# A gated layer with quantised down projection on one core: a planner with chance and room, weight ranges by sums of absolute values, and a shorter rounding of the down weights

## The chip, the cores and the metric

The kernel runs on one core of a Trainium2 chip. A core has five engines that work side by side and meet at semaphores: TensorE (PE) multiplies matrices, and its loads of stationary operands (PEld) overlap the multiplications; VectorE (DVE), ScalarE (ACT) and GpSimd (POOL) work on elements; SyncE (SP) issues transfers between the chip's memory and the on-chip buffer. Each engine takes its own instructions in the order in which they were emitted. Results of TensorE land in eight banks of an accumulator memory (PSUM), which the other engines read.

The metric is the device time of one execution in microseconds, smaller is better. Three runs of the kernel before took 744.97, 745.54 and 746.1; their median is 745.54.

## What is computed

The reference, cut to what matters (B = 4 batches of S = 1024 tokens, D = 512, FF = 2048, C = 128):

```python
scale = cond @ norm_w.T + 1.0
ms = jnp.mean(x * x, axis=-1, keepdims=True)
h = x * (scale[:, None, :] * jax.lax.rsqrt(ms + EPS))
u = h @ up_w.T
val, gate = jnp.split(u, 2, axis=-1)
h = val * jax.nn.gelu(gate, approximate=False)
hq = h + jax.lax.stop_gradient(act_quant(h) - h)            # 127 / max|h| of a token, rounded
wq = down_w + jax.lax.stop_gradient(weight_quant(down_w) - down_w)   # -1, 0 or 1 by the mean of |w|
y = hq @ wq.T
return y + x
```

So each token is normalised, goes through a gated layer, has its 2048 values rounded to whole numbers by its own largest value, and is multiplied with a matrix of -1, 0 and 1.

## The kernel before

**Tiles.** The 2048 rows of the hidden layer are 16 tiles of 128 (index `j`), each with a gate and a value half of `up_w`. Tokens of a batch are two halves of 512. A slot `g = 16 b + j` is one row tile of one batch. The up products are done in 16-bit floats, each operand split into a high and a low part (`w_high`, `w_low`, `s_high`, `s_low`, `Tokens.high`, `Tokens.low`). Batch 0 uses the plain product (`plain`, `plain_half`, L886; the very first is `plain_first`, L929); later batches use seven products of half size with sums of blocks (`product`, L871, called from `slot`). The down product uses the same scheme in `Pair` (L1142) and, for the last batch, a plain one (`down_mm`, L1091).

**Preparing weights.** While batch 0 is computed, each row tile of `up_w` is loaded into H (`w_load`, L570 and L573), its range is found (`w_largest`, L578: the largest absolute value of each row; `w_factor`, L456 to L587: down to a power of two, a factor and its reciprocal), it is scaled (`w_scale`: GpSimd L606 for tiles 0 to 5, ScalarE L604 for tiles 6 to 15), and turned, either by TensorE through banks po (`w_turn`, L614, evacuated by `w_high`, `w_low`, `w_evac`) or, from tile 6 on, by a transposing transfer (`w_rows`, L628 to L630). GpSimd forms the sums of blocks (`s_sums`, L662 to L665), ScalarE and GpSimd split them (L674, L678), and SyncE stores them in memory (L682), from where later batches load them again. A row's factor only has to be a power of two that keeps the parts inside the 16-bit range; `gain` takes it out again.

`down_w` is loaded in eight pieces (`d_load`, L729), summed in absolute value by ScalarE (`d_sum`, L733), and rounded to -1, 0, 1: VectorE takes two steps (`d_round`, L748 and L749) and ScalarE writes the result as 8-bit floats (`d_put`, L758); a transposing transfer puts them into `wd` (L760), and VectorE forms block sums (`d_sums`, L771).

**A slot.** In batch 0 a half is: a gate product into bank A or B, Gelu by ScalarE (L910), a value product into bank E, their product by VectorE into H (L914), which frees bank E. In later batches a slot has six products in banks A, B and E, copies of A and E by ScalarE (L949, L957, L961), two Gelus (L966, L982) and sums by VectorE (L969, L979, L985, L988). VectorE keeps a running largest value of each token over pairs of tiles (`pair_max`: L1000, L1005, L1007).

**Change of batch.** When a batch's last pair is in, GpSimd takes the maximum over partitions (`token_max`, L1021, an all-reduce, with an empty one ahead of it, `get_ready`, L1014), VectorE makes the scale from it (`token_scale`: L1026, four reciprocals L1032 for each half), and 16 pieces are scaled and rounded (`quant_scale`, L1063; `quant_round`, L1067, or ScalarE L1071 and L1075), in the first half of the next batch's slots. Meanwhile the next tokens are squared, scaled and split (`Tokens.norm`, L805, L775, L776; `Tokens.scale`, L813, L815).

**The planner.** No engine call is emitted where it is written. `Engine` records it, and `Plan` adds it as a step with its dependences (by the parts of tiles that it reads and writes), a price (`price`) and, for a transfer, a time on the DMA engines. `Plan.order` repeats 24 times: `needed` works back from the end to when each step is due, `place` puts the steps, earliest due first, into the first room on their engine, and `replay` runs the resulting order through the prices. The order with the earliest end of TensorE is emitted, engine by engine. So a change of a price or of a rule of the planner can move every instruction of the kernel.

Of the kernel before, what the change touches and what calls it, by code (L numbers as in the profile page):

```python
# [21 lines left out]
P = 128  # L22
# [5 lines left out]

W_UP = 2.0**12
X_UP = 2.0**8  # L30

# [79 lines left out]
class Plan:  # L111


    def __init__(self):
        self.steps = []
        self.wrote, self.read = {}, {}
        self.loaded = {}
        self.lines = {}
# [5 lines left out]
    def add(self, eng, method, real, args, kwargs):  # L124
# [48 lines left out]
        s.deps = deps  # L173
        self.steps.append(s)

    def order(self):

        steps = self.steps
        for s in steps:
            s.after, s.cost = [], (s.alone + s.beside) / 2  # L180
        for s in steps:
            for d in s.deps:
                steps[d].after.append(s)
        clock = 0.0
        for s in steps:
            if s.eng == "PE":
                s.start = clock
                clock += s.cost
        best = None
# [17 lines left out]
    def place(self):  # L207

        steps = self.steps
        used = {e: Line() for e in ("PE", "ACT", "DVE", "POOL", "SP", "DMA")}  # L210
        last = 0.0
# [12 lines left out]
    def replay(self, order):  # L224

# [3 lines left out]
        for s in order:  # L229
# [11 lines left out]
            s.cost = (s.cost + cost) / 2 if e in port else cost  # L241
            free[e] = s.end
            if s.wait:
                free["DMA"] = max(free["DMA"], t + ISSUE) + s.wait
                s.end = free["DMA"] + LANDING
        return free["PE"]

# [6 lines left out]

ROUNDS, ISSUE, LANDING, RELOAD = 24, 1.2, 1.5, 6.5

# [28 lines left out]
def price(eng, method, writes, reads, args, kwargs):  # L285
# [72 lines left out]
def glu_quant_kernel(  # L358
# [34 lines left out]
    DVE.memset(one, 1.0)  # L393
    ones = one.to_broadcast([P, P])


# [42 lines left out]
    )  # L439
    A21 = R[:, 0, 6144 : 6144 + 768].bitcast(F16).rearrange("p (n w f) -> p n w f", n=3, w=2)  # L440

    def s_tile(g):
# [132 lines left out]
    def w_largest(j, t0=0, t1=2):  # L575
        t = slice(t0, t1)
        am = sm.tile([P, 2], F32, name=f"wam_{j}_{t0}", tag="wam")[:, t]
        DVE.tensor_reduce(am, wn(j)[:, t], AX.X, ALU.max, apply_absolute_value=True)  # L578
# [167 lines left out]
    def d_round(n):  # L746
        dn = d_part(n)
        DVE.tensor_scalar(dn, dn, wsc, 1.0, ALU.mult, ALU.min)  # L748
        DVE.tensor_scalar(dn, dn, -1.0, MAGIC, ALU.max, ALU.add)  # L749

    tn = []

    def d_put(n):
# [3 lines left out]
        t8 = tn[-1].bitcast(F8).rearrange("p (f y) -> p f y", y=2)  # L757
        ACT.activation(t8[:, :, y], d_part(n), AF.Copy, bias=-MAGIC, saturate=False)  # L758
        if y:
# [1118 lines left out]
```

## Time and profile before

| | before |
|---|---|
| median of three runs | 745.54 us |
| profiled execution, its own time | 746.14 us |
| its span in the trace | 744.4 us |
| ScalarE, VectorE, GpSimd busy | 392.7, 606.1, 210.5 us |
| DMA: read and written | 58.93 MB and 23.09 MB |
| DMA: packets under 512 bytes | 141750 of 179567 |

The profiled execution's own time is 1.7 us longer than its span, for what lies around the program. Rows of groups read: line, engine, operation, output and input with their shapes, count, then the busy time in us, the mean duration in ns, and the idle time of the engine just before them with what ended it. Rows of a timeline read: start, duration, engine, line, operation, shapes, count, and in brackets the idle time of the engine before it and what ended that. A matmul's duration holds its way through the pipeline, so successive ones overlap.

### The profile page before, as it was taken

What the parts mean: (1) busy time and instruction counts of PE and PEld (TensorE: products, weight loads), DVE (VectorE), ACT (ScalarE), POOL (GpSimd) and SP (SyncE); (2) the same over time, 40 slices, a digit from 0 to 9 for tenths busy, and PEclk for the clock granted to TensorE, in tenths of its full rate; (3) what the DMA queues carried; (4) which work ended last, traced back from release to release, by engine and by line L of the source; (5) the groups of instructions that cost most, each with busy time, mean ns of one, the idle gap of its engine ahead of it and who ended that gap; (6) DMA issues with size and microseconds to landing.
All of it is one profiled execution on the core that took longest, in us unless ns stands there. A gap on an engine that the chain in (4) does not pass through costs nothing.

```text
span 744.4 us, 10218 instructions
## 1 busy us (share of the span) xinstructions
PE 725.6 (97%) x3684; PEld 362.5 (49%) x3684; DVE 606.1 (81%) x833; ACT 392.7 (53%) x635; POOL 210.5 (28%) x213
## 2 busy tenths in 40 slices
PE   6999999999979999999999999999999999999997
PEld 3544444444434445666444445566444444445744
DVE  6787899988988887977587888988579889755897
ACT  5787576565225688333334678623333665332363
POOL 1775887857223034300015003800001000000000
PEclk9999999999999999999999999999999999999999
DMA  9838688899423454768733454676833344443514
GB/s 305 334 87 267 226 222 220 194 248 233 139 68 99 125 138 120 176 178 193 202 101 100 100 131 124 161 199 153 192 122 102 100 103 104 107 103 89 153 48 151
DMA packets 179567, 115.74 MB, mean 155 GB/s; under 512 B 141750, under 2 KB 147767, under 8 KB 179516
## 3 DMA queue, kind: packets, MB, share of 16 engines
q1 hardware_dynamic: 179226, 114.76, 57.5%
q10 hardware_dynamic: 290, 0.33, 0.3%
q8 instruction: 29, 0.48, 0.3%
q14 instruction: 22, 0.18, 0.1%
HBM read 58.93 MB, written 23.09 MB: 110 GB/s over the span
## 4 chain that ended last, share of the span: by engine, by line
PE 78%; DVE 9%; POOL 4%; issue 3%; ACT 3%; DMA 1%; SPq 0%; DVEq 0%; POOLq 0%; ACTq 0%
PE A L871 31%; PE E L871 15%; PE po L1142 8%; PE B L871 8%; PE E L886 5%; PE B L886 2%; PE A L886 2%; PE po L1091 2%; PE E L1091 1%; PE A L1091 1%; DMA H<-in_x_dram 1%; DVE H L629 1%; POOL H L663 1%; DVE nx L854 1%; DVE wam L578 1%
## 5 line engine op out<-in xcount | busy, mean ns | idle before, releaser
L871 PEld LDWEIGHTS <-SXY 128*128 128x128 f16 x2016 | 197.3, 98 | 237.1 <-issue 5.8
L871 PE MATMUL A<-R,SXY 128*128 128x512 f16 x1152 | 266.4, 379 | 3.7 <-ACT t L949 1.6
L871 PE MATMUL E<-R,SXY 128*128 128x512 f16 x576 | 140.0, 379 | 0.8 <-DVE t L979 0.8
L1021 POOL PARTITION_ALL_REDUCE am<-R x8 | 18.9, 2364 | 304.3 <-DVE R L1007 286.4
L1063 DVE TENSOR_TENSOR H<-H,am 128x1024 f32<-128x1024 f32 x64 | 78.3, 1256 | 0.2
L886 PEld LDWEIGHTS <-SXY 128*128 128x128 f16 x462 | 45.2, 98 | 55.6 <-issue 2.1
L969 DVE SCALAR_TENSOR_TENSOR H<-A,sg,t 128x512 f32<-128x512 f32 x48 | 35.9, 749 | 43.0 <-PE A L871 42.9
L871 PE MATMUL B<-R,SXY 128*128 128x512 f16 x288 | 70.0, 379 | 0.0
L1005 DVE TENSOR_REDUCE gm<-H 128x512 f32<-128x1024 f32 x56 | 69.0, 1232 | 1.0
L982 ACT ACTIVATE t<-t,sg 128x512 f32<-128x512 f32 x48 | 34.7, 722 | 54.6 <-DVE t L979 54.6
L949 ACT COPY t<-A 128x512 f32<-128x512 f32 x48 | 28.1, 585 | 60.0 <-PE A L871 60.0
L1142 PE MATMUL po<-wd,R 128*128 128x256 fp8e4 (+1 forms) x448 | 56.8, 275 | 0.8 <-ACT po L1168 0.8
L957 ACT COPY B<-A 128x512 f32<-128x512 f32 x48 | 27.4, 570 | 51.4 <-PE A L871 51.4
L1142 PEld LDWEIGHTS <-R 128*128 128x128 bf16 (+1 forms) x480 | 47.0, 98 | 13.9 <-issue 1.3
L985 DVE TENSOR_TENSOR v<-A,v 128x512 f32<-128x512 f32 x48 | 33.2, 691 | 24.9 <-PE A L871 22.4
L966 ACT ACTIVATE t<-B,sg 128x512 f32<-128x512 f32 x48 | 33.0, 687 | 32.6 <-PE B L871 32.0
L886 PE MATMUL E<-R,SXY 128*128 128x512 f16 x210 | 49.9, 379 | 0.0
L979 DVE TENSOR_TENSOR t<-E,t 128x512 f32<-128x512 f32 x48 | 33.0, 687 | 20.4 <-PE E L871 19.7
L886 PEld LDWEIGHTS <-R 128*128 128x128 f16 x282 | 27.5, 98 | 34.4 <-issue 2.0
L1071 ACT ACTIVATE H<-H 128x1024 f32<-128x1024 f32 x38 | 40.0, 1051 | 7.5 <-DVE H L1063 7.3
L961 ACT COPY v<-E 128x512 f32<-128x512 f32 x48 | 28.1, 586 | 28.4 <-PE E L871 21.5
L1007 DVE TENSOR_TENSOR R<-R,gm 128x512 f32<-128x512 f32 x56 | 40.4, 722 | 1.4
(232 smaller groups left out, 1036.9 us busy)
## 6 DMA issues: line engine op xcount, KB each, us to landing
SXY<-s_dram SPq DMA_DIRECT2D x66, 256.0 KB, 2.7
SXY<-s_dram SPq DMA_DIRECT2D x18, 384.0 KB, 3.9
H<-in_L_cond_up_w_dram SPq DMA_DIRECT2D x13, 512.0 KB, 5.5
s_dram<-SXY SPq DMA_DIRECT2D x14, 384.0 KB, 4.0
xr<-in_x_dram SPq DMA_DIRECT2D x19, 256.0 KB, 3.7
out_dram<-xr SPq DMA_DIRECT2D x19, 256.0 KB, 2.0
H<-in_x_dram SPq DMA_DIRECT2D x8, 512.0 KB, 5.3
R<-in_L_cond_down_w_dram SPq DMA_DIRECT2D x8, 512.0 KB, 7.4
```

The lines of the kernel that those rows point to most:

```text
L871: PE.matmul(o, s[:, w, k, :], tv[:, :, c, l, k, :], start=start and n == 0, stop=stop and n == len(TERMS) - 1, skip_group_check=True,)
L886: PE.matmul(ps, a[k // 2][:, w, k % 2, :], XP[:, l, k, h * TOK : (h + 1) * TOK], start=n == 0, stop=n == len(terms) - 1,)
L966: ACT.activation(cur["t1"], pb, AF.Gelu, scale=gain(g, 1))
L969: DVE.scalar_tensor_tensor(h_half(g - 1, 0), prev["A"], gain(g - 1, 0), prev["t1"], ALU.mult, ALU.mult)
L979: DVE.tensor_tensor(prev["t2"], prev["E"], prev["t2"], ALU.add)
L982: ACT.activation(prev["t2"], prev["t2"], AF.Gelu, scale=gain(g - 1, 1))
L985: DVE.tensor_tensor(cur["v"], cur["A"], cur["v"], ALU.add)
L1005: DVE.tensor_reduce(gm[0], v, AX.X, ALU.max, apply_absolute_value=True)
L1007: return [largest, lambda: DVE.tensor_tensor(m, m, gm[0], ALU.max)]
L1063: DVE.tensor_tensor(v, v, r.to_broadcast([P, 2, TOK]), ALU.mult)
L1071: ACT.activation(v, v, AF.Copy, bias=MAGIC)
L1142: PE.matmul(po, w[:, j], m, start=start and j == 0, stop=stop and j == n - 1, skip_group_check=True,)
```

## The change

Five things change.

- `w_largest` for tiles 6 to 15 (`BY_SUM`): instead of one VectorE reduction to the largest absolute value, two ScalarE activations write the absolute values of 512 elements to a scratch place and give their sum; the factor in `w_factor` is doubled for them (`W_UP_SUM`).
- `d_round`: VectorE multiplies and adds the rounding constant in one step, with no clamps; `d_put` takes the sign after subtracting the constant, instead of a copy.
- Planner, dependences: among the first 150 steps (`HEAD`) each step that is not a transfer follows the one written before it on its engine.
- Planner, placing: TensorE's steps may go into room between others; other steps are placed with some room after their inputs (0, 0.3, 0.6 or 0.9 us in turn, at most a tenth of what they have until due); a transfer's place is found on the DMA engines first. Among 25 rounds the order is chosen by the mean end over four replays in which costs (TensorE's apart) and landings are drawn at random, and the end is that of all steps.
- Planner, prices: ScalarE, GpSimd and VectorE prices are adjusted a little.

The diff, cut to its core:

```diff
@@ add
+        if not s.wait:
+            if s.n < HEAD and eng in self.last:
+                deps.add(self.last[eng])
+            self.last[eng] = s.n
@@ order
+        best, chance = None, random.Random(1)
         for n in range(ROUNDS):
             self.needed(clock)
-            self.place()
+            self.place(0.3 * (n % 4))
             order = sorted(steps, key=lambda s: (s.start, s.n))
             clock = self.replay(order)
-            if best is None or clock < best[0]:
-                best = clock, order
+            late = sum(self.replay(order, chance) for _ in range(MISSES)) / MISSES
+            if best is None or late < best[0]:
+                best = late, order
+            self.replay(order)
@@ needed
-            s.late = clock if s.eng != "PE" else s.start
+            s.late = s.start if s.eng == "PE" else clock - s.cost
@@ place
-            if s.eng == "PE":
-                t = max(t, last)
-                last = t + s.cost
-                s.start, s.end = t, last
-                continue
+            if s.eng != "PE":
+                t += min(margin, max(0.0, s.late - t) * 0.1)
+            if s.wait and s.eng == "SP":
+                t = used["DMA"].put(t + ISSUE, s.wait) - ISSUE
             s.start = used[s.eng].put(t - s.before, s.before + s.cost) + s.before
-            s.end = s.start + s.cost
-            if s.wait:
-                s.end = used["DMA"].put(s.start + ISSUE, s.wait) + s.wait + LANDING
+            s.end = s.start + (ISSUE + s.wait + LANDING if s.wait else s.cost)
@@ replay
+            if chance:
+                cost *= 1.0 if e == "PE" else 0.95 + 0.14 * chance.random()
+            else:
+                s.cost = (s.cost + cost) / 2 if e in port else cost
...
-        return free["PE"]
+        return max(s.end for s in order)
...
+HEAD = 150
+ROUNDS, MISSES, ISSUE, LANDING, RELOAD = 25, 4, 1.2, 1.5, 6.5
@@ price
-        cost = 0.06 + wide * 0.0009 + (0.07 if method != "copy" else 0)
+        cost = 0.08 + wide * 0.0009 + (0.05 if method != "copy" else 0) + (0.05 if psum else 0)
...
-        return cost, cost * 1.33, 0.0
+        return cost, cost * 1.42, 0.0
...
-    return cost, cost * (1.35 if method == "scalar_tensor_tensor" else 1.65), 0.0
+    return cost, cost * (1.35 if method == "scalar_tensor_tensor" else 1.8), 0.0
@@ w_largest, w_factor
+        if j >= BY_SUM:
+            for n in range(t0, t1):
+                ACT.activation(w_junk, wn(j)[:, n], AF.Abs, accum_out=am[:, n : n + 1])
+            return am
         DVE.tensor_reduce(am, wn(j)[:, t], AX.X, ALU.max, apply_absolute_value=True)
...
-        DVE.tensor_scalar(sw[:, j, t], am, 2.0**-100, 1.0 / W_UP, ALU.max, ALU.mult)
+        up = W_UP_SUM if j >= BY_SUM else W_UP
+        DVE.tensor_scalar(sw[:, j, t], am, 2.0**-100, 1.0 / up, ALU.max, ALU.mult)
@@ d_round, d_put
-        DVE.tensor_scalar(dn, dn, wsc, 1.0, ALU.mult, ALU.min)
-        DVE.tensor_scalar(dn, dn, -1.0, MAGIC, ALU.max, ALU.add)
+        DVE.tensor_scalar(dn, dn, wsc, MAGIC, ALU.mult, ALU.add)
...
-        ACT.activation(t8[:, :, y], d_part(n), AF.Copy, bias=-MAGIC, saturate=False)
+        ACT.activation(t8[:, :, y], d_part(n), AF.Sign, bias=nmagic, saturate=False)
```

More of the change, by code (lines that the diff above doesn't have):

```diff
@@ L1 @@
 import bisect
+import random
 import sys
@@ L29 @@
 W_UP = 2.0**12
+BY_SUM = 6
+W_UP_SUM = 2.0**13
 X_UP = 2.0**8
@@ L116, in __init__ @@
         self.wrote, self.read = {}, {}
-        self.loaded = {}
+        self.loaded, self.last = {}, {}
         self.lines = {}
@@ L188, in order @@
                 clock += s.cost
-        best = None
+        best, chance = None, random.Random(1)
         for n in range(ROUNDS):
             self.needed(clock)
-            self.place()
+            self.place(0.3 * (n % 4))
             order = sorted(steps, key=lambda s: (s.start, s.n))
             clock = self.replay(order)
-            if best is None or clock < best[0]:
-                best = clock, order
+            late = sum(self.replay(order, chance) for _ in range(MISSES)) / MISSES
+            if best is None or late < best[0]:
+                best = late, order
+            self.replay(order)
         self.replay(best[1])
@@ L202, in needed, with place, replay @@
         for s in reversed(self.steps):
-            s.late = clock if s.eng != "PE" else s.start
+            s.late = s.start if s.eng == "PE" else clock - s.cost
             for t in s.after:
                 s.late = min(s.late, t.late - lag(s, t) - s.wait - s.cost)
-    def place(self):
+    def place(self, margin):
         steps = self.steps
         used = {e: Line() for e in ("PE", "ACT", "DVE", "POOL", "SP", "DMA")}
-        last = 0.0
         for s in sorted(steps, key=lambda s: (s.late, s.n)):
             t = max((steps[d].end + lag(steps[d], s) for d in s.deps), default=0.0)
-            if s.eng == "PE":
-                t = max(t, last)
-                last = t + s.cost
-                s.start, s.end = t, last
-                continue
+            if s.eng != "PE":
+                t += min(margin, max(0.0, s.late - t) * 0.1)
+            if s.wait and s.eng == "SP":
+                t = used["DMA"].put(t + ISSUE, s.wait) - ISSUE
             s.start = used[s.eng].put(t - s.before, s.before + s.cost) + s.before
-            s.end = s.start + s.cost
-            if s.wait:
-                s.end = used["DMA"].put(s.start + ISSUE, s.wait) + s.wait + LANDING
-    def replay(self, order):
+            s.end = s.start + (ISSUE + s.wait + LANDING if s.wait else s.cost)
+    def replay(self, order, chance=None):
         steps = self.steps
@@ L239, in replay @@
                 port[e] = t + cost
+            if chance:
+                cost *= 1.0 if e == "PE" else 0.95 + 0.14 * chance.random()
+            else:
+                s.cost = (s.cost + cost) / 2 if e in port else cost
             s.start, s.end = t, t + cost
-            s.cost = (s.cost + cost) / 2 if e in port else cost
             free[e] = s.end
-            if s.wait:
+            if s.wait and e != "SP":
+                s.end = t + ISSUE + s.wait + LANDING
+            elif s.wait:
                 free["DMA"] = max(free["DMA"], t + ISSUE) + s.wait
-                s.end = free["DMA"] + LANDING
-        return free["PE"]
+                s.end = free["DMA"] + LANDING + (chance.random() if chance else 0.0)
+        return max(s.end for s in order)
     def emit(self, steps):
@@ L252, in emit @@
             call(s.do, s.args, s.kwargs)
-ROUNDS, ISSUE, LANDING, RELOAD = 24, 1.2, 1.5, 6.5
+HEAD = 150
+ROUNDS, MISSES, ISSUE, LANDING, RELOAD = 25, 4, 1.2, 1.5, 6.5
 class Line:
@@ L394, in glu_quant_kernel @@
     ones = one.to_broadcast([P, P])
+    nmagic = cpool.tile([P, 1], F32, name="nmagic")
+    DVE.memset(nmagic, -MAGIC)
     R = cpool.tile([P, 2, NA * 2048], F32, name="R")
@@ L440, in glu_quant_kernel @@
     A21 = R[:, 0, 6144 : 6144 + 768].bitcast(F16).rearrange("p (n w f) -> p n w f", n=3, w=2)
+    w_junk = R[:, 0, 5888:6144].bitcast(BF16)
     def s_tile(g):
```

## The prediction

> **What bounds the kernel now.** I read the page's busy times first, then the busy time of each engine in stretches, then TensorE's timeline for the places where it idled, and last the other engines' timelines around those places.
>
> ```profile
> span 744.4 us, 10218 instructions
> ...
> PE 725.6 (97%) x3684; PEld 362.5 (49%) x3684; DVE 606.1 (81%) x833; ACT 392.7 (53%) x635; POOL 210.5 (28%) x213
> ```
>
> TensorE is busy for 97% of the span, so this is a TensorE-bound kernel, and a change that leaves its matmuls alone can win at most the time in which it stands still. The windows say where that is (columns: PE, PEld, DVE, ACT, POOL busy with counts, granted clock, DMA share, GB/s):
>
> ```profile
> 0.00:25.00 25.00, 18.59 (x81) 9.49 (x82) 16.44 (x66) 15.31 (x33) 4.49 (x11) 0.93 0.94 328
> 25.00:60.00 35.00, 33.66 (x173) 17.10 (x172) 29.07 (x57) 26.93 (x53) 30.23 (x34) 1.00 0.54 184
> 60.00:140.00 80.00, 80.00 (x377) 36.93 (x376) 69.65 (x94) 51.35 (x82) 61.41 (x63) 1.00 0.79 225
> 140.00:200.00 60.00, 58.27 (x270) 26.30 (x269) 54.03 (x66) 29.95 (x50) 34.04 (x34) 1.00 0.89 214
> 200.00:226.00 26.00, 21.56 (x98) 9.47 (x97) 21.52 (x29) 9.35 (x18) 8.00 (x7) 1.00 0.31 82
> 226.00:740.00 514.00, 513.24 (x2692) 263.21 (x2690) 414.57 (x526) 259.78 (x401) 72.28 (x68) 1.00 0.51 131
> ```
>
> TensorE loses 6.4 us up to 25, where first loads set the pace, 1.3 up to 60, 1.7 in 140 to 200, 4.4 in 200 to 226 where batch 0 gives way to batch 1, and 0.8 in the 514 us after that. VectorE is busy 87% of 60 to 140 and 90% of 140 to 200, with ScalarE at 64% and 50%.
>
> ```profile
> 13.19 0.55 PE L1231 MATMUL po<-ident,H 128*128 128x128 f32 x3 [2.74 <-DVE wam L456]
> ...
> 37.91 0.38 PE L886 MATMUL A<-R,SXY 128*128 128x512 f16 x1 [0.17 <-ACT R L1235]
> ...
> 39.65 2.10 PE L886 MATMUL A<-R,SXY 128*128 128x512 f16 x9 [0.20 <-ACT R L1235]
> ...
> 44.88 1.33 PE L614 MATMUL po<-ident,H 128*128 128x128 f32 x8 [0.54 <-POOL H L606]
> ...
> 143.63 2.53 PE L886 MATMUL B<-R 128*128 128x512 f16 x11 [1.73 <-ACT t L910]
> ...
> 200.69 2.75 PE L871 MATMUL A<-R,SXY 128*128 128x512 f16 x12
> 203.28 1.46 PE L871 MATMUL E<-R,SXY 128*128 128x512 f16 x6
> ...
> 207.26 2.75 PE L871 MATMUL A<-R,SXY 128*128 128x512 f16 x12 [1.22 <-DVE v L985]
> ...
> 213.50 1.45 PE L871 MATMUL A<-R,SXY 128*128 128x512 f16 x6 [0.91 <-DVE H L969]
> 215.72 1.46 PE L871 MATMUL E<-R,SXY 128*128 128x512 f16 x6 [0.76 <-DVE t L979]
> ...
> 223.91 2.32 PE L871 MATMUL A<-R,SXY 128*128 128x512 f16 x10 [1.56 <-ACT t L949]
> ...
> 303.70 1.47 PE L1142 MATMUL po<-wd,R 128*128 128x256 fp8e4 x11 [0.25 <-ACT po L1168]
> ...
> 489.71 1.47 PE L1142 MATMUL po<-wd,R 128*128 128x256 fp8e4 x11 [0.51 <-ACT po L1168]
> ```
>
> A bracket counts from the end of a matmul's pipeline, but a matmul can start before the last one has drained: the twelve at 200.69 end at 203.44, while the next starts at 203.28. So each stall cost 0.16 us more than its bracket. Four waits for L1235 (37.91 to 39.65) and one for L606 come to 1.3 + 5 x 0.16 = 2.1; the wait at 143.63 to 1.9; the four at the change of batch to 4.45 + 0.64 = 5.1; the last two to 0.76 + 0.32 = 1.1. Together 10.2 us behind the first 25.
>
> What stood behind those waits is an engine that works in order and was late or blocked:
>
> ```profile
> 36.44 0.83 ACT L674 CAST SXY<-H 128x768 f16<-128x768 f32 x1 [1.36 <-POOL H L663]
> ...
> 142.59 0.41 ACT L674 CAST R<-H 128x256 f16<-128x256 f32 x1 [4.60 <-POOL H L665]
> 142.90 0.68 ACT L910 ACTIVATE t<-B,sg 128x512 f32<-128x512 f32 x1
> ...
> 302.65 0.72 ACT L982 ACTIVATE t<-t,sg 128x512 f32<-128x512 f32 x1 [3.15 <-DVE t L979]
> ```
>
> At 36.44 and 142.59 a cast of weight sums (L674) waits for GpSimd, and behind it in ScalarE's queue stand the copies of L1235 and the Gelu that frees bank B. At 302.65 a Gelu waits for VectorE and holds up the copy of L1168. At the change of batch it is VectorE's backlog:
>
> ```profile
> 201.09 3.39 DVE L1032 RECIPROCAL am<-am 128x128 f32<-128x128 f32 x4
> ...
> 206.52 0.68 DVE L985 TENSOR_TENSOR v<-A,v 128x512 f32<-128x512 f32 x1
> ...
> 209.17 3.16 POOL L1021 PARTITION_ALL_REDUCE am<-R  x1 [9.42 <-DVE R L1007]
> 220.16 0.18 POOL L775 TENSOR_SCALAR ssq<-ssq 128x2 f32<-128x2 f32 x1 [7.83 <-issue]
> ...
> 221.47 0.72 ACT L813 ACTIVATE xn<-xn,rs 128x512 f32<-128x512 f32 x1 [3.59 <-POOL rs L776]
> ```
>
> The step that TensorE needs (L985) comes after four reciprocals and more. The second token maximum starts 9.42 us late because VectorE's pair maximum (L1007) is late; GpSimd then needs 7.83 us before its next ordinary operation, and ScalarE, waiting for that result (L813), keeps back the copy of L949 for which TensorE waits 1.56.
>
> **The change part by part.** *Less VectorE work in batch 0.*
>
> ```profile
> L578 DVE TENSOR_REDUCE wam<-H 128x2 f32<-128x1024 f32 x15 | 18.1, 1208 | 0.6 <-DMA H<-in_L_cond_up_w_dram 0.6
> L748 DVE TENSOR_SCALAR R<-R,wsc 128x1024 f32<-128x1024 f32 x8 | 9.4, 1174 | 0.0
> L749 DVE TENSOR_SCALAR R<-R 128x1024 f32<-128x1024 f32 x8 | 7.4, 935 | 0.1
> L758 ACT ACTIVATE v<-R 128x1024 fp8e4<-128x1024 f32 x8 | 8.2, 1052 | 3.1 <-DVE R L749 3.1
> L805 ACT ACTIVATE xt<-xn 128x512 f32<-128x512 f32 x12 | 7.5, 622 | 0.4 <-DVE gm L1005 0.4
> L805 ACT ACTIVATION_READ_ACCUMULATOR xt<-xn 128x1 f32 x12 | 2.3, 189 | 0.0
> ```
>
> Row tiles 6 to 15 lose the reduction of L578: 10 x 1.208 = 12.1 us. The rounding of down_w keeps one of its two steps: 8 x 0.935 = 7.4 us. Of VectorE's 69.65 + 54.03 us in 60 to 200 these 19.5 are 16%; it would be busy 74% of that stretch instead of 88%. ScalarE takes twenty sums of absolute values of 128 x 512 instead. The nearest row is the squares of L805, equal in shape and with an accumulator to read: between 0.62 (the reading hidden) and 0.81 (all of it behind); I take 0.73, 14.6 us in all. ScalarE's 51.35 + 29.95 of those 140 us become 96, or 68%, so there is room, but in an in-order queue the two sums of a tile can hold up a Gelu by 1.5 us. The sign takes the place of the copy with a bias (L758), same shape, same engine; the changed program holds two table loads like the old one, so no function asks for one more. At twice the 622 of a square of half the width a sign would cost 1244 against 1052, 1.5 us in all, and ScalarE's idle third hides it; at the copy's own price 0, which I take, for the shape is the same. If ScalarE had no room there, all of these sums would add to the path; that is a rival below.
>
> *A new order.* This is the larger part: what the planner now puts where. Of the instructions that both programs share, about four in ten change place on VectorE, three in ten on ScalarE, GpSimd and SyncE, and one in seven on TensorE, whose matmuls are the same ones. Place by place:
>
> At the change of batch, VectorE does the last pair maxima (L1005, L1007) of both halves before the first scale step (L1026), so GpSimd's two all-reduces stand one behind the other and the 7.83 us begin up to 9.4 us earlier, the length of that wait. Between L1026 and the first L985 stand three reciprocals, 2.5 us, where four, a quantization and more took 5.9 (200.64 to 206.52 in the trace). Two of the four waits lose their cause outright (L985 and L949 behind L813), and the other two (L969, L979) had been pushed by the same backlog. What may stay: ScalarE's squares and rescalings of the next tokens still stand ahead of one copy into bank B, and one L813 of 0.72 can show there: 0.5. So 4.6 of the 5.1 go; bounds 2.6 (only the two with a cause undone, 1.38 + 1.72 = 3.1, less that 0.5) and 5.1.
>
> At 37 to 40 the four copies of L1235 now stand directly behind a Gelu, and the cast that waited for GpSimd stands behind them; the scaling of w that the transposes at 44.88 wait for comes earlier too. 2.1 goes, bounds 1.0 and 2.1. At 143.63 the Gelu has no cast waiting for GpSimd ahead of it: 1.9 goes, bounds 0 and 1.9. At 303.70 and 489.71 the copy of L1168 now stands ahead of the Gelu that waited: 1.0 of 1.1 goes.
>
> A new wait: near tile 6 VectorE has two pair maxima in a row ahead of L914, which frees bank E.
>
> ```profile
> L1005 DVE TENSOR_REDUCE gm<-H 128x512 f32<-128x1024 f32 x56 | 69.0, 1232 | 1.0
> L1007 DVE TENSOR_TENSOR R<-R,gm 128x512 f32<-128x512 f32 x56 | 40.4, 722 | 1.4
> ```
>
> Queued are 1.23 + 1.23 + 0.72 = 3.2 us. Their first two thirds pass while the Gelu that L914 reads is still being made; I charge the rest, 1.2, bounds 0 and 3.2.
>
> *The first 150 steps in written order.* The zeros for the warm-up matmuls are now written after the identity, so TensorE begins about 1 us later, against nothing but warm-up. The reduction of L578 stands ahead of the square-root steps and waits for its load, not for them; that takes some 0.6 us (half of 1208) out of the way of L1226, ahead of the wait at 13.19. Against this, the range of tile 1 (1.2 + 0.5 us of small steps) now stands ahead of the low halves that the last matmuls of the first product need, and the table load for Gelu moves from an idle place to one between copies:
>
> ```profile
> L1300 ACT ACT_TABLE_LOAD x1 | 1.3, 1283 | 0.0
> ```
>
> That load is hidden by the dozen matmuls that read halves copied before it; uncovered it costs 1.3. I take a gain of 0.3 for the head, bounds +1.5 and -1.5.
>
> The Trainium skill, in "TensorE: Matmul & The Clock Gate", "What's actually happening", says that the array runs at half clock until a free-running window of about 3.4 us was busy and falls back after an idle one. The granted clock of 0.93 up to 25 us agrees. By that rule the later warm-up could move one half-speed window, which is worth up to 1.7 us either way by its figure; it is no part of my sum.
>
> *DMAs.* All 360 transfers of SyncE stay. Most loads of down_w move from 10 to 13 us to behind the loads of up_w, and they are first read by ScalarE's sums 20 us on. SyncE's queue is in order too: a spill of weight parts that waits for GpSimd holds the up_w load behind it.
>
> ```profile
> DMA to landing us min/median/max: 3.8/5.5/12.9
> ```
>
> These landings are of L570. The slowest, 12.9, was issued right behind three scattered stores of the condition rows; the new order puts that load ahead of them. I charge 0, bounds 0 and 3, for the ScalarE sums wait directly for these loads.
>
> **The sum.** 4.6 + 2.1 + 1.9 + 1.0 + 0.3 - 1.2 = 8.7. The old order had eleven waits with a mean of 10.2 / 11 = 0.9; I leave one such for the new order: 7.8. The profiled execution took 746.14 (span 744.4, and 1.7 around it), so 738.3 on its terms; the median of the runs, 745.54, lies 0.6 under it, and 745.54 - 7.8 = 737.7.
>
> **Rivals.** *Waits that move* (chance 0.15): the backlog is pushed rather than removed, since pair maxima and column sums of down_w are pulled forward into the room that was made, and TensorE waits at bank E or B in several new places. For it: VectorE is still busy three quarters of that stretch. Against it: the new order shows one such pile-up only. Half of the gain stays: 745.5 - 3.9 = 741.6. *The order does not matter* (0.05): the waits at the change of batch are the chain of maximum, scale and quantization itself, and the others shrink by chance; then 745. Against it speaks that between those steps VectorE did work of other pairs. *ScalarE becomes the bound* (0.06): a tile's sums stand in its queue waiting for an up_w load that SyncE holds behind a spill; the Gelus and copies behind them stop TensorE. It decides once a landing plus its delay passes some 13 us, 7.5 over the median; each further microsecond is lost whole, for up to ten tiles. At 1 us for each tile: 737.7 + 10 = 747.7, slower than before. Against it: the row shows 5.5 as the median. *All waits go* (0.10): without the charges of 1.2 and 0.9 and with the clock's or head's gain, 735.
>
> **How the numbers follow.** The forecast, 737.7, has 0.64; its own range is 735.5 to 740.5. The range that should hold 8 in 10 takes in the case above it and most of the one below: 734.5 to 742.5. A change of 0.2%, 1.5 us, is about what a measurement of this kernel can tell from none. The forecast, the moved waits and the case without waits are all faster: 0.89, with a little of "the order does not matter" 0.90; the rest of that one is no change, 0.04; ScalarE as the bound is slower, 0.06.
>
> **What would show it.** Right: no TensorE wait over 0.6 us between 190 and 225; the two all-reduces of the first change of batch back to back; 19 us less on VectorE and 15 more on ScalarE before 200; about 10 us of matmul gaps behind the first 25 turned into 2 or 3. Wrong: waits for L914 or for Gelus at tiles 6 to 15 in place of the old ones, ScalarE idle for up_w loads, or a second half-speed stretch in the first 25 us.

## The result, and the profile after

The changed kernel took 737.92 us (median; 737.77 to 738.88) beside 745.47 us (744.97 to 746.10) before: a ratio of 0.9901, with a 95% interval of 0.9884 to 0.9918. The forecast was 737.7. The profiled execution took 737.95 us, its span 736.2.

The head of the page, and the busy time by stretches (columns as before: PE, PEld, DVE, ACT, POOL busy with counts, granted clock, DMA share, GB/s):

```profile
span 736.2 us, 10220 instructions
...
PE 723.5 (98%) x3684; PEld 361.9 (49%) x3684; DVE 600.0 (82%) x816; ACT 406.3 (55%) x675; POOL 218.1 (30%) x213
```

```profile
0.00:25.00 25.00, 19.01 (x87) 9.40 (x88) 16.60 (x67) 15.37 (x34) 3.15 (x8) 1.00 0.75 251
25.00:60.00 35.00, 35.00 (x184) 18.53 (x183) 32.21 (x60) 30.55 (x61) 27.88 (x33) 1.00 0.87 245
60.00:140.00 80.00, 79.95 (x377) 36.86 (x375) 69.57 (x90) 61.13 (x110) 65.09 (x63) 1.00 0.90 217
140.00:200.00 60.00, 60.00 (x279) 27.09 (x277) 50.31 (x56) 34.50 (x61) 42.33 (x38) 1.00 0.92 231
200.00:226.00 26.00, 26.00 (x122) 11.82 (x121) 21.65 (x28) 12.82 (x20) 7.72 (x8) 1.00 0.38 101
```

From 25 to 226 TensorE now loses 0.05 us, where before it lost 1.3, 0, 1.7 and 4.4. VectorE is as busy as before from 60 to 140 (69.57 us, before 69.65), though a good part of its work there is gone; the experiments come back to this.

What TensorE still waits for (columns: engine, tile and line, what it waited for; us in total, times, longest), and its timeline at two places:

```profile
PE A L1269 <- DVE eps L1209: 3.6, 1, 3.6
PE A L893 <- DVE H L991: 2.0, 2, 1.6
PE po L1253 <- DVE wam L474: 1.1, 1, 1.1
...
PE po L1164 <- ACT po L1190: 0.5, 1, 0.5
```

```profile
23.25 1.03 PE L908 MATMUL A<-R,SXY 128*128 128x512 f16 x4
...
478.00 0.81 PE L893 MATMUL A<-R,SXY 128*128 128x512 f16 x3 [1.65 <-DVE H L991]
```

Behind 25 us one wait of weight is left, at 478.00, in a place where the old order had none. What VectorE did ahead of it is work of the next tokens and of the down product:

```profile
473.55 1.48 DVE L876 TENSOR_TENSOR H<-H 128x256 f16<-128x256 f32 x1
474.95 2.34 DVE L1140 TENSOR_TENSOR H<-R 128x1024 bf16<-128x1024 bf16 x2
477.21 0.74 DVE L991 SCALAR_TENSOR_TENSOR H<-A,sg,t 128x512 f32<-128x512 f32 x1
```

The books: the same 3684 matmuls run from 2.10 (start of the first) to 740.03 (start of the last) before, and from 3.58 to 731.87 now. So 9.6 us of delay between them went, of which the later start of the first takes back 1.5. A stall below is the time by which a matmul starts later than is usual after one of the kind ahead of it (0.215 us after 128x512, for example). Behind 25 us the stalls over 0.3 us went from 10.2 to 3.0 (1.81 at 478, 0.70 at 463, 0.53 at 403).

GpSimd at the change of batch, and the groups whose price the prediction had estimated (columns: line, engine, operation, shapes, count; busy us, mean ns; idle before them):

```profile
191.69 1.81 POOL L1043 PARTITION_ALL_REDUCE am<-R  x1 [1.29 <-DVE R L1029]
193.68 1.92 POOL L1043 PARTITION_ALL_REDUCE am<-R  x1 [0.18 <-DVE R L1029]
203.45 0.18 POOL L797 TENSOR_SCALAR ssq<-ssq 128x2 f32<-128x2 f32 x1 [7.85 <-ACT v L983]
```

```profile
L598 ACT ACTIVATE R<-H 128x512 bf16<-128x512 f32 x20 | 12.5, 627 | 1.9 <-DMA H<-in_L_cond_up_w_dram 1.4
L598 ACT ACTIVATION_READ_ACCUMULATOR R<-H 128x1 f32 x20 | 3.7, 187 | 0.0
L780 ACT ACTIVATE v<-R,nmagic 128x1024 fp8e4<-128x1024 f32 x8 | 9.0, 1145 | 1.5 <-DVE R L771 1.5
...
L771 DVE TENSOR_SCALAR R<-R,wsc 128x1024 f32<-128x1024 f32 x8 | 10.0, 1291 | 0.0
L1010 DVE SCALAR_TENSOR_TENSOR H<-v,sg,t 128x512 f32<-128x512 f32 x48 | 41.5, 865 | 2.9 <-ACT t L1004 2.7
```

The two all-reduces stand one behind the other, and the 7.85 us that GpSimd needs before its next ordinary operation end at 203 instead of 220.

### The profile page after: what moved, and what is told of

Same layout as the page of the kernel before. It is cut to its first block, busy times and chain, and to the rows that moved or that the text cites. A ratio compares the mean times of both kernels' runs of the same rounds, so it can differ in the third digit from the quotient of the medians.

```text
span 736.2 us, 10220 instructions
## 1 busy us (share of the span) xinstructions
PE 723.5 (98%) x3684; PEld 361.9 (49%) x3684; DVE 600.0 (82%) x816; ACT 406.3 (55%) x675; POOL 218.1 (30%) x213
## 4 chain that ended last, share of the span: by engine, by line
PE 89%; DVE 7%; DMA 1%; ACT 1%; POOL 1%; issue 1%; SPq 0%; DVEq 0%; ACTq 0%
PE A L893 32%; PE E L893 16%; PE E L908 11%; PE B L893 8%; PE po L1164 8%; PE A L908 6%; PE B L908 5%; DVE H L1085 3%; DMA H<-in_x_dram 1%; PE po L637 1%; DVE H L1010 1%; DVE R L1122 1%; DVE R L1089 1%; PE B L1164 0%; PE A L1113 0%
## 5 line engine op out<-in xcount | busy, mean ns | idle before, releaser
L893 PE MATMUL A<-R,SXY 128*128 128x512 f16 x1152 | 270.8, 379 | 2.0 <-DVE H L991 2.0
L893 PE MATMUL E<-R,SXY 128*128 128x512 f16 x576 | 143.2, 379 | 0.0
L1043 POOL PARTITION_ALL_REDUCE am<-R x8 | 15.4, 1924 | 274.1 <-DVE R L1029 274.1
L1164 PE MATMUL po<-wd,R 128*128 128x256 fp8e4 (+1 forms) x448 | 58.9, 275 | 0.5 <-ACT po L1190 0.5
L908 PE MATMUL E<-R,SXY 128*128 128x512 f16 x210 | 49.7, 379 | 0.0
L1007 DVE TENSOR_TENSOR v<-A,v 128x512 f32<-128x512 f32 x48 | 33.1, 690 | 18.7 <-PE A L893 17.9
L1010 DVE SCALAR_TENSOR_TENSOR H<-v,sg,t 128x512 f32<-128x512 f32 x48 | 41.5, 865 | 2.9 <-ACT t L1004 2.7
```

Source lines behind the costliest of these rows:

```text
L893: PE.matmul(o, s[:, w, k, :], tv[:, :, c, l, k, :], start=start and n == 0, stop=stop and n == len(TERMS) - 1, skip_group_check=True,)
L908: PE.matmul(ps, a[k // 2][:, w, k % 2, :], XP[:, l, k, h * TOK : (h + 1) * TOK], start=n == 0, stop=n == len(terms) - 1,)
L1007: DVE.tensor_tensor(cur["v"], cur["A"], cur["v"], ALU.add)
L1010: DVE.scalar_tensor_tensor(h_half(g - 1, 1), prev["v"], gain(g - 1, 0), prev["t2"], ALU.mult, ALU.mult)
L1164: PE.matmul(po, w[:, j], m, start=start and j == 0, stop=stop and j == n - 1, skip_group_check=True,)
```

## The experiments

The theory at the start was the prediction's: the gain is mostly the new order, for which less VectorE work makes room. The rivals: the relief itself is the gain, whatever the planner does; or a single rule of the planner does it. Each ratio below is to the kernel before in the same set of runs, with its 95% interval. In the four sets the kernel before took 745.47 to 745.88 us, so differences of times between sets are good to about half a microsecond.

**Work and planner apart.** `e1_new_work_old_planner` is the kernel before with the new sums and the new rounding alone, planned anew by the old planner with its old prices. `e2_old_work_new_planner` is the changed kernel with the old work put back:

```diff
-        if j >= BY_SUM:
-            for n in range(t0, t1):
-                ACT.activation(w_junk, wn(j)[:, n], AF.Abs, accum_out=am[:, n : n + 1])
-            return am
...
-        DVE.tensor_scalar(dn, dn, wsc, MAGIC, ALU.mult, ALU.add)
+        DVE.tensor_scalar(dn, dn, wsc, 1.0, ALU.mult, ALU.min)
+        DVE.tensor_scalar(dn, dn, -1.0, MAGIC, ALU.max, ALU.add)
...
-        ACT.activation(t8[:, :, y], d_part(n), AF.Sign, bias=nmagic, saturate=False)
+        ACT.activation(t8[:, :, y], d_part(n), AF.Copy, bias=-MAGIC, saturate=False)
```

> The changed kernel's work (ten tiles' ranges by ScalarE's sums, down_w rounded in one VectorE step and a sign), ordered by the planner of before with its prices. Theory (relief and order together): the old planner leaves the written head and the blocked casts as they were, but has 19.5 us less VectorE work to place before the change of batch, so about half of the gain: 741 to 743. Rival 'order alone': no gain, 745. Rival 'work alone': all of it, 738.

> The work of before, ordered by the changed planner. Theory (relief and order together): the waits of casts ahead of Gelus go, the backlog at the change of batch stays in part: 740 to 743. Rival 'order alone': 738. Rival 'work alone': 745.

Measured: e1 741.69 us, ratio 0.9938 (0.9922 to 0.9954); e2 738.06 us, 0.9898 (0.9883 to 0.9912). e1 came out as its theory had it, e2 as the rival 'order alone'. The planner alone gives the whole gain; under the new planner the lighter work adds nothing that the intervals can tell. Under the old planner it gives 4.2 us, about half. So the two do not add up: each is a way to much the same waits. TensorE's timeline of e1 at the change of batch still has the last of the four waits, behind L961 (before L949), and nearly all of the others are gone:

```profile
220.13 2.75 PE L883 MATMUL A<-R,SXY 128*128 128x512 f16 x12 [1.66 <-ACT t L961]
```

e2 (its profiled execution took 740.22) has all of VectorE's old work and no wait over 0.3 us at the change of batch; its longest behind 25 us is one for bank E in batch 0:

```profile
79.53 1.02 PE L897 MATMUL E<-R 128*128 128x512 f16 x4 [2.49 <-DVE H L925]
...
80.53 4.44 PE L897 MATMUL B<-R 128*128 128x512 f16 x12
```

The second row is longer than the 2.75 of every other such dozen; more on that below.

**Order and work apart.** e1 and e2 both plan anew, so they do not tell load from order. The next two hold an order still, on every engine, and change the work in it: `e3_old_order_new_work` plans the kernel before and puts the new instructions in the places of the old ones when they are emitted; `e4_new_order_old_work` does the reverse with the changed kernel's order (the VectorE reduction stands where the second of the two sums stood).

```diff
-            call(s.do, s.args, s.kwargs)
+            for do, args, kwargs in [(s.do, s.args, s.kwargs)] if s.n not in SWAP else SWAP[s.n](s):
+                call(do, args, kwargs)
...
+            SWAP[len(book.steps)] = lambda s: [
+                (nc.scalar.activation, (w_junk, wn(j)[:, n], AF.Abs), {"accum_out": am[:, n : n + 1]})
+                for n in range(t0, t1)
+            ]
...
+        SWAP[len(book.steps)] = lambda s: [(s.do, (dn, dn, wsc, MAGIC, ALU.mult, ALU.add), {})]
+        SWAP[len(book.steps)] = lambda s: []
```

> Every engine's order of before held, with the changed work put in place: at the place of each of the ten reductions ScalarE gets the two sums, the second rounding step is left out, the copy becomes a sign. Theory: VectorE reaches the change of batch up to 19.5 us earlier, so the four waits there (5.1) shrink, while the waits at 37 to 45 (2.1), 303 and 489 (1.1) stay, and ScalarE's sums, now at places that were not planned for them, hold up some Gelus: 741 to 744. Rival 'order alone': 745 or more. Rival 'work alone': 738.

> Every engine's order of the changed kernel held, with the work of before put back: VectorE reduces at the place of each tile's sums and rounds in two steps, ScalarE copies instead of taking the sign. 19.5 us come back onto VectorE in an order that has no room planned for them. Theory: stalls at banks E and B come back before the change of batch: 741 to 746. Rival 'order alone': 738.

Measured: e3 744.56 us, 0.9981 (0.9970 to 0.9992); e4 747.88 us, 1.0021 (1.0008 to 1.0033). Both lie above the ranges that were expected. e3 is the run that decides on "backlog". Its page, one group, its stretch from 60 to 140, and TensorE at the change of batch:

```profile
PE 725.2 (98%) x3684; PEld 362.0 (49%) x3684; DVE 585.1 (79%) x816; ACT 406.0 (55%) x675; POOL 208.3 (28%) x213
```

```profile
L1010 DVE SCALAR_TENSOR_TENSOR H<-v,sg,t 128x512 f32<-128x512 f32 x48 | 36.2, 753 | 1.1 <-ACT t L1004 1.0
```

```profile
60.00:140.00 80.00, 80.00 (x377) 36.94 (x376) 55.14 (x80) 60.95 (x113) 62.17 (x64) 1.00 0.84 231
```

```profile
204.85 2.75 PE L893 MATMUL A<-R,SXY 128*128 128x512 f16 x12 [1.37 <-DVE v L1007]
...
211.09 1.46 PE L893 MATMUL A<-R,SXY 128*128 128x512 f16 x6 [0.90 <-DVE H L991]
213.31 1.46 PE L893 MATMUL E<-R,SXY 128*128 128x512 f16 x6 [0.76 <-DVE t L1001]
...
221.50 2.75 PE L893 MATMUL A<-R,SXY 128*128 128x512 f16 x12 [1.55 <-ACT t L971]
```

VectorE has 21.0 us less to do than before, and is busy 69% of that stretch. Yet the four waits are the four of before, with brackets of 1.37, 0.90, 0.76 and 1.55 where they were 1.22, 0.91, 0.76 and 1.56. They are no backlog carried over from before: VectorE stands at the wrong instruction at that moment, however idle it was until then. Only the wait at 143.63 went with the load (from 1.9 to 0.24).

The same rows hold a second surprise. e3 and the changed kernel issue the same 816 VectorE instructions, and take 585.1 and 600.0 us for them. The order alone makes VectorE 14.9 us slower: L1010, for one, takes 865 ns in the mean against 753. GpSimd's 213 take 218.1 against 208.3. In the faster kernel more of the two engines' work falls together: its VectorE instructions spend 211 us beside a busy GpSimd, those of e3 176. Of the 48 of L1010, those with no GpSimd instruction beside them last 744 ns in both kernels (37 and 40 of them), those with GpSimd busy for over half of their time 1316 ns (10) and 838 (5).

e4 loses 10 us against the changed kernel. One row of its waits, and VectorE there:

```profile
PE E L923 <- DVE H L951: 4.2, 5, 2.7
```

```profile
79.77 1.22 DVE L606 TENSOR_REDUCE wam<-H 128x2 f32<-128x1024 f32 x1 [2.60 <-DMA H<-in_L_cond_up_w_dram]
80.91 0.74 DVE L951 SCALAR_TENSOR_TENSOR H<-E,sg,t 128x512 f32<-128x512 f32 x1
```

Put back on VectorE, the reduction waits for its load with L951 behind it, for which TensorE waits. An order is good for the work that it was made with.

**Which of the planner's rules.** Four kernels, each the changed one less one rule, planned anew: TensorE strictly in the order of its due times, as in the old planner (`e5_pe_in_due_order`), no room behind inputs (`e6_no_margin`), the order picked by one replay without drawn costs (`e7_no_chance`), and no written order at the start (`e8_no_head`).

```diff
+            if s.eng == "PE":
+                t = max(t, last)
+                last = t + s.cost
+                s.start, s.end = t, last
+                continue
```

```diff
-            self.place(0.3 * (n % 4))
+            self.place(0.0)
```

```diff
-            late = sum(self.replay(order, chance) for _ in range(MISSES)) / MISSES
+            late = clock
...
-            self.replay(order)
```

```diff
-HEAD = 150
+HEAD = 0
```

> The changed kernel, but the planner again puts TensorE's steps strictly one behind the other by due time, as before; all else of the changed planner stays. Theory (the freedom of TensorE's order carries the gain, because a matmul that is ready goes ahead of one that waits): 741 to 745. Rival 'room and chance carry it': 738. Rival 'the written head carries it': 738.

> The changed kernel, planner without the room after a step's inputs (margin always 0), chance kept. Theory (freedom of TensorE's order): 737.5 to 739. Rival 'room and chance carry it': 741 to 744. Rival 'the written head': 738.

> The changed kernel, planner that picks the order by the end of one replay without drawn costs; room kept. Theory (freedom of TensorE's order): 737.5 to 739.5. Rival 'room and chance carry it': 740 to 744. Rival 'the written head': 738.

> The changed kernel, planner without the rule that keeps the first 150 steps in written order. In the trace of after the first product of tile 1 starts at 23.25 instead of 24.52, 1.3 us earlier, and the granted clock shows no half-speed stretch after 10 us. Theory: only that goes, 738.5 to 739.5. Rival 'the written head carries it': 741 or more.

Measured: e5 737.28 us, 0.9891 (0.9872 to 0.9911); e6 758.44 us, 1.0168 (1.0151 to 1.0185); e7 743.77 us, 0.9970 (0.9951 to 0.9988); e8 739.55 us, 0.9917 (0.9902 to 0.9932). The intervals of e5 and e8 overlap the changed kernel's (0.9884 to 0.9918), so neither TensorE's freedom nor the written start is shown to be worth anything. e7 is 5.9 us slower than the changed kernel, and e6, without the room, 13 us slower than the kernel before.

Three limits of this. e7's edit also leaves out the second replay of each round, which corrects the prices, so its 5.9 us belong to both. Each rule is judged by a single plan, and e11 below differs by 5.3 us from the changed kernel with every rule in place and one price changed; so 5.9 is not shown to be the rule's. For the room two plans speak, e6 and e12. And the changed prices, the DMA engines looked at first and the end taken over all steps have no run of their own.

e8's result has two parts that work against each other: its first plain product starts at 25.07 instead of 23.25, with half clock from 12.09 to 18.92 (the granted clock of all four runs is 0.994 or 0.995, that of three of the changed kernel's four 1.000), and its stalls over 0.3 us behind 25 us come to 1.6 instead of 3.0.

The longest waits of e6 and e7 have one face: something that ScalarE needs from memory is late. SyncE's queue and ScalarE in e6, the DMAs there, and TensorE's wait:

```profile
55.39 0.46 SPq L558 DMA_DIRECT2D rows_dram<-scT  x1
...
61.67 0.38 SPq L588 DMA_DIRECT2D H<-in_L_cond_up_w_dram  x1
62.10 0.93 SPq L558 DMA_DIRECT2D rows_dram<-scT  x1
```

```profile
79.57 0.63 ACT L598 ACTIVATE R<-H 128x512 bf16<-128x512 f32 x1 [10.33 <-DMA H<-in_L_cond_up_w_dram]
```

```profile
74.00:78.00 4.00, 3.17 (x15) 1.26 (x13) 0.00 (x0) 0.00 (x0) 0.00 (x0) 1.00 0.76 54
```

```profile
PE E L908 <- DVE H L936: 10.9, 2, 9.1
```

By the semaphore for which ScalarE waits, its load of `up_w` is the one issued at 61.67 (not the next, of 68.65, which the expectation of e9 names). It lands at 79.55, 17.9 us after its issue, where the median of these loads is 4.2. ScalarE's sum waits 10.33, and TensorE 9.1. This is the prediction's rival "ScalarE becomes the bound" as a mechanism, in an order that was not the changed kernel's. In e7 a spill is late instead, issued at 60.49, half a microsecond behind such a store, and landing 14.6 us later:

```profile
75.14 0.59 ACT L660 CAST R<-po 128x512 f16<-128x512 f32 x1 [5.40 <-DMA s_dram<-R]
```

**The scattered stores.** Ahead of both late transfers in SyncE's queue stand stores of a condition row (`rows_dram`), 512 pieces of four bytes each, which the planner prices at 1.4 us on the DMA engines. A new theory: they cost what the room was protecting against. In `e9_no_margin_stores_later` (e6's order) and `e10_stores_later` (the changed kernel's order) the stores of rows 2 and 3 are emitted right ahead of the loads that read them; in `e11_scatter_price` and `e12_no_margin_scatter_price` the planner is told a price of 4.1 us for each and plans anew.

```diff
+        if b > 1:
+            SWAP[len(book.steps)] = lambda s: [
+                (s.do, (), {"out": rows_dram[b].rearrange("(k p) -> p k", p=P), "in_": scT[:, :, b]}),
+                (s.do, s.args, s.kwargs),
+            ]
```

```diff
+        if last < 64 and str(out.space).endswith("DRAM"):
+            return 0.45, 0.0, nbytes / 0.5e3
```

> The order of the planner without room (e6, 758.4) held on every engine, but the scattered stores of the condition rows of batches 2 and 3 (2 KB in 512 pieces each) are emitted right ahead of the loads that read them, one batch and two batches on. In e6 the up_w load issued at 68.65 landed near 79.5 with ScalarE idle 10.3 and TensorE 9.1 us behind it, at 54 GB/s. Theory (the store ahead of it blocks the transfers for some 4 us and the order has no room for that): that wait goes, with the half-speed stretch after it: 744 to 749. Rival (VectorE's or ScalarE's queue order itself makes the wait): 756 or more.

> The changed kernel's order held, with the same two stores moved behind. In the trace of after its up_w loads land in 8.1 us at most and ScalarE waits 0.4 us for the one behind the stores. Theory: nothing to win on TensorE, 737 to 738. Rival (the stores cost the changed kernel too): 736 or less.

> The changed kernel with one more price corrected in the planner: a transfer that stores single elements is priced at 2 KB per 4.1 us instead of 1.4, after the 12 us for three in the trace of before. The whole order is planned again. Theory: about the same, 736 to 739, since the room has taken up the difference already. Rival (the wrong price costs the changed kernel): 734 to 736.

> The planner without room (e6, 758.4) with the corrected price of scattered stores, planned again. Theory (room is worth what the planner's prices miss, and this price was the largest miss): 740 to 747. Rival (room is needed whatever the prices): 752 or more.

Measured: e9 763.35 us, 1.0243 (1.0229 to 1.0257); e10 755.52 us, 1.0146 (1.0129 to 1.0163); e11 743.19 us, 0.9966 (0.9956 to 0.9977); e12 762.37 us, 1.0223 (1.0209 to 1.0237). All four theories miss. e9 lies where its rival had put it, but for another reason, as shown below. e12 lies where its rival had put it, and leaves that rival standing: room is needed whatever the prices, as far as a price that was still too low can tell. e10's miss is the clearest. SyncE, ScalarE and TensorE of e10 in a row, and the DMAs behind the other store, issued at 316.72, in a stretch in which it stood alone:

```profile
187.84 0.61 SPq L574 DMA_DIRECT2D rows_dram<-scT  x1
198.57 0.33 SPq L574 DMA_DIRECT2D sc<-rows_dram  x1
...
199.42 0.43 SPq L830 DMA_DIRECT2D xn<-in_x_dram  x1
...
206.12 0.63 ACT L838 ACTIVATE xt<-xn 128x512 f32<-128x512 f32 x1 [10.48 <-DMA xn<-in_x_dram]
...
207.99 1.44 PE L904 MATMUL B<-R,SXY 128*128 128x512 f16 x3 [9.31 <-ACT B L990]
```

```profile
319.00:322.00 3.00, 3.00 (x20) 1.73 (x19) 2.97 (x5) 1.18 (x3) 1.90 (x2) 1.00 0.08 5
322.00:325.00 3.00, 3.00 (x16) 1.35 (x15) 2.76 (x6) 1.74 (x3) 0.00 (x0) 1.00 0.00 0
```

The load that reads a store is issued 10.7 us after it, and until then SyncE, which works in order, issues nothing: the load of the next tokens behind it comes late, ScalarE's squares wait, the copy L990 behind them waits, TensorE waits 9.31. So the move made the price visible: 10 us for 2 KB, of which the last 6 and more move next to nothing. In e9 it did remove the wait that it was meant for (e6's 9.1 us; the longest for that bank is now 2.6), and it put another of 10.2 us at the change of batch, for the same reason: VectorE waits 8.10 us there for the load of the row. So the cure failed, and the cause of e6's wait stands: with the two stores gone from that place, the two loads of `up_w` that took 17.9 and 14.9 us in e6 land in 5.5 us each.

e11 shows the same with a price that is too low: planned at 4.1 us, the store has its load issued 15 us behind it, and VectorE, in whose queue the scaling of that row stands, idles. (In e12 it idles 20.2 us in all behind the three rows' loads.)

```profile
442.46 0.57 SPq L560 DMA_DIRECT2D rows_dram<-scT  x1
...
457.42 0.33 SPq L565 DMA_DIRECT2D sc<-rows_dram  x1
...
462.30 0.49 DVE L569 TENSOR_SCALAR sc<-sc,ux 128x512 f32<-128x512 f32 x1 [6.13 <-DMA sc<-rows_dram]
...
466.16 0.59 PE L895 MATMUL A<-R,SXY 128*128 128x512 f16 x2 [4.75 <-ACT t L973]
```

What a price of 10 us, or a store without scattering, would give was not tried. No run came out faster than the changed kernel by more than the intervals; e5's 737.28 is not told apart from it.

## Why the prediction was right

The number held: 7.8 us were forecast from the median shown, and 745.47 less 737.92 is 7.6. So did the main mechanism, that the larger part is the new order; e2, e3 and e4 show it. Two slips in the working change nothing: the waits listed are twelve, not eleven (a mean of 0.85), and a third of 3.2 is 1.1, not 1.2. By its steps:

- *Change of batch, 4.6 gone.* All of 5.1 went; 26.00 of 26.00 us are busy, and the all-reduces are back to back as the order promised.
- *37 to 45, 2.1; 143.63, 1.9; 303.70 and 489.71, 1.0 of 1.1.* The first two went whole; of the kind of the third, a wait for L1190 (before L1168) is left at another place, 0.5 in its bracket.
- *The new wait near tile 6, charged 1.2.* It is 0.2 at most: no stall above 0.21 lies between 25 and 226. Charged too much.
- *One unknown wait, 0.9.* It came, as the one of 1.81 at 478.00, with two of 0.70 and 0.53 besides. What the sum had kept back or charged, 0.5 + 0.1 + 1.2 + 0.9 = 2.7, stands against 3.0 measured: too much for tile 6 and too little for the unknown ones. That these nearly cancel is luck.
- *The head, 0.3.* The first plain product starts at 23.25 instead of 24.52. That is 1.27, but hardly the new order: in e3, with the old order, it starts at 23.47 (the rows below are the kernel before's and e3's). The difference is the granted clock up to 25 us, 0.93 before and 1.00 in both others, which the prediction had left out of its sum as the window's chance. In the profile before, half clock lasts from 15.04 to 18.45, behind a wait that took 2.74 us there (the prediction's row at 13.19) and 1.3 in e3, which has the same order. The Trainium skill, "TensorE: Matmul & The Clock Gate", "What's actually happening", has the window run free of the kernel; the starts of such stretches, in the last section, agree. So 1.05 (24.52 less 23.47) of the 8.2 us by which the profiled execution is shorter are likely no merit of the change, and 0.2 is left for the head. The medians hardly hold this 1.05: of the 43 later runs of the kernel before, 40 have a granted clock of 0.999 or 1.000, against 0.998 in the profiled one.

```profile
24.52 1.67 PE L886 MATMUL A<-R,SXY 128*128 128x512 f16 x7
```

```profile
23.47 2.75 PE L908 MATMUL A<-R,SXY 128*128 128x512 f16 x12
```

- *ScalarE's sums and the sign.* 627 and 187 ns for each sum, 16.2 us where 14.6 were charged (ScalarE's total rose by 13.6, since such ends overlap); the sign 1145 against 1052 ns, 0.7 us in all, between the two bounds. ScalarE's idle time hid both: e2, without them, is no faster.
- *"Less VectorE work makes room."* This is the step that was wrong, though the sum didn't rest on it. The 12.1 us of reductions went, and 6.8 of the 7.4 for rounding (16.8 to 10.0), but VectorE's total fell by 6.1 only, from 606.1 to 600.0, since the new order makes other instructions longer. From 60 to 140 the room was filled up again. e2 needs no relief for the gain, e3 has all the relief and gains 1.3 us (745.88, the kernel before on the same chip, less 744.56). What the waits at the change of batch wanted was not time but place. So one of the prediction's own signs failed: VectorE was to have 19 us less before 200, and has 0.5 less (168.70 us, before 169.18); ScalarE was to have 15 more, and has 18.0.
- *The rivals.* "The order does not matter" fell by e3 and e4: the new work takes 6.6 us more in the old order (744.56 less 737.92), and the old work 9.8 more in the changed kernel's order than in its own (747.88 less 738.06). "Waits that move" is there in small, at 478.00. "ScalarE becomes the bound" did not happen here (its sums waited 1.4 us in all), and e6 shows that it would cost more than was reckoned: 9.3 us of wait for one tile, and 2.0 more by half clock behind it.

## What to carry to other kernels

Where engines work in order, ask of a stall not how busy the late engine is but at which instruction its queue stood, and hold the order still while taking work away before calling anything a backlog: e3 took 21 us from VectorE and left four waits as they were. With estimated prices, slack behind inputs was worth more here than lighter work: both plans without it (e6, e12) are slower than the plan of the kernel before. In e6 the longest wait goes back to a price that fell far short, 1.4 us for a 2 KB store whose load was issued some 10 us later in e9 and e10; a price of 4.1 us did not replace the room (e12). What judging an order under drawn costs is worth stays open; a difference of 5 us between two plans says little about the rule between them, since one price moved a plan as far (e11). A planned order belongs to its work: steps exchanged or moved in a finished order cost 10 us in e4, 18 in e10 and 5 in e9, and won 1.3 in e3. After a change of a step plan anew.

## What was not expected of the hardware

*The clock drops after waits of over 2.3 us.* Behind the first 25 us, each wait of TensorE of over 2.3 us in these traces (counted as the stalls above) came with a stretch at half clock of 3.41 us or a multiple of it, which began during it or within 2 us of its end; the shortest were 2.33 (e7) and 2.50 us (e6). None of the waits up to 2.18 us did, unless it lay in such a stretch already. The dozen of 4.44 us in e2 above is one; the granted clock of e2 there, and a dozen of e12 behind the wait of 2.18 (2.00 in its bracket), show the difference:

```profile
80.80:84.20 3.40, 3.40 (x10) 1.25 (x9) 2.54 (x4) 0.83 (x1) 3.40 (x4) 0.52 0.76 141
```

```profile
151.61 2.75 PE L910 MATMUL B<-R,SXY 128*128 128x512 f16 x12 [2.00 <-ACT t L934]
```

Where TensorE is busy throughout, a stretch of 3.41 us costs 1.7 (4.44 instead of 2.75 in e2), so a wait of 2.5 us costs 4.2, as an estimate from these two; a stretch that begins during the wait costs less. In every trace with more than one such stretch the starts lie whole multiples of 3.413 us apart: 20 in e4, 40 in e6, 21 and 58 in e9, 39 in e10, 28 and 81 in e12. So the clock changes on a grid that runs through the whole execution. The Trainium skill, "TensorE: Matmul & The Clock Gate", "What's actually happening", has the clock fall back after a window of about 3.4 us without work; here less than a whole window did it.

*A store of 512 pieces of four bytes takes 10 us* until the load that reads it is issued (9.9 to 10.7 in e9 and e10, 15 in e11), though in e10 the last piece of the store of 316.72 starts before 319 and the DMA engines then stand nearly still (0.08 and 0.00 of the share above). Other transfers feel it: in e6 512 such pieces go out at 60 to 62 us and 502 at 71 to 72, and right behind each of the two, packets of 7168 bytes, 0.28 us in the median of that trace, last up to 6.9 us. What holds them up is not shown.

*The same VectorE instructions took 585.1 or 600.0 us*, by how much GpSimd worked beside them (the numbers of L1010 stand with e3).
